# Eight PSUM banks for the first graph layer, and a hand-ordered tail with part of its rows on ScalarE and GpSimd

## The chip, the cores and the metric

The kernel runs on one core of a Trainium2 chip, in float32 almost throughout. The time is device microseconds (us) of that core, the median of several executions. Engines are named as the profile names them: PE (TensorE matmuls), PEld (TensorE weight loads), DVE (VectorE), ACT (ScalarE), POOL (GpSimd), SP (SyncE, which here only issues DMAs).

## What is computed

One transformer-like block over 1250 nodes with 768 features and 20000 edges. Cut to what matters:

```python
xn = layernorm(x)
x  = x + gnn(xn, edges) + linear_attention(xn)     # gnn: two graph attention layers, then @ Wu
y  = layernorm(x)
shared = silu(y @ ws_gate) * (y @ ws_up) @ ws_down
routed = sum over the 2 best of 8 experts of gate * expert(y)
out = x + alpha * shared + (1 - alpha) * routed     # alpha = sigmoid(y @ sg_w + sg_b)
```

A graph attention layer weighs, for each target node and head, the source nodes' rows by a softmax over the incoming edges: `out[dst] = sum(alpha * h[src])`. The first layer has 4 heads, the second 2.

## The kernel before, in words

Tokens are cut into ten tiles of 125 rows (`NT = 10`, `TP = 125`). `acc` (125 x 10 x 768, in SBUF) holds the running sum of the block and in the end the output. The stages follow each other: weights and counts of edges, linear attention, first graph layer, second graph layer with the product by Wu, routing, 22 blocks of expert work, and the tail. The order of instructions within each engine is set by a scheduler that keeps to dependencies; it may move instructions of one engine past each other, and each engine then runs its own list strictly in order. Waits are kept per tile: a write into a tile waits for the earlier reads of that tile, also when they touch another half of it. Two stages are touched.

**First graph layer** (`attend`, L582 to L603, with `step1` and `finish1`, L613 to L624). It runs over two halves of the targets (625 each) and four heads, so eight rounds, called heads below. A head takes ten steps, one for each tile of source nodes. In a step ACT makes two exponentials `ea` and `eb` (L593, L595; two buffers each), DVE takes their maximum (L596) and multiplies it by the edge counts into `u` (L598; three buffers), and PE adds u times G into five PSUM tiles `pa` (L615), one for each tile of 125 targets. A tile `pa` takes one of the eight PSUM banks. One `nc.tensor.matmul` of float32 shows as two MATMUL records, so a step is ten records, a head a hundred. When a head's ten steps are in, DVE takes for each of the five `pa` a reciprocal (L622) and a scaled sum into `h2` (L623), after which the bank is free. The pool `g1ps` (L612) has `NH2` = 5 banks: exactly one head's. Two further banks (`ps_m`, L444) are kept through both graph layers for small transposes `m_row` (L456), among them the ten that turn `h2` columns into the rows which the second layer starts from (`g_srow`, then a DMA out, a broadcast DMA back, and twenty maxima on DVE, L480).

**Tail** (L1108 to L1136). The expert blocks have scattered their rows into `ys` in DRAM. Ten DMAs on the SP queue (L1112) fetch for each token tile the two routed rows, `yg`, 768 KB each. For tiles 2 to 9, PE multiplies the shared expert's hidden rows by ws_down into `pds` (`shared`, L1047 to L1055): a tile `pds` has two halves of 384 columns in two banks, three tiles are in use, and a half is three matmuls (six records). DVE adds each half times `al` to `acc` (L1054). For each tile u, DVE adds its two routed rows times their gates (L1131), 768 columns each. A tile that is done is stored by two DMAs, 120 rows from the SP queue and 5 from the ACT queue (`store`, L1117 and L1118). Which of L1054 and L1131 comes first on DVE is left to the scheduler. The DMAs of SP and ACT take turns on eight completion semaphores, and a DMA waits until the one before it on its semaphore has landed.

Earlier in the kernel, GpSimd adds a bias to `acc` tile by tile (L402), 125 x 768 as well; VectorE works beside it.

Of the kernel before, what the change touches and what calls it, by code (L numbers as in the profile page):

```python
# [14 lines left out]
AF = mybir.ActivationFunctionType  # L15
ALU = mybir.AluOpType
AX = mybir.AxisListType
PSUM = bass.MemoryType.PSUM

P = 128  # L20
TP = 125
NT = 10
# [3 lines left out]
HALF = D // 2  # L26
# [35 lines left out]
def gps_block(ctx: ExitStack, tc: tile.TileContext, x, src, dst, norm_g, norm_b, W1, a_src1, a_dst1, b1,  # L62
              W2, a_src2, a_dst2, b2, Wu, bu, w_qkv, w_proj, b_proj, router_w, w_gate, w_up, w_down,
              ws_gate, ws_up, ws_down, sg_w, sg_b, out):
    nc = tc.nc
# [11 lines left out]
    acc = big.tile([TP, NT, D], F32, name="acc")  # L77
# [12 lines left out]
    ctx_g = ExitStack()  # L90
# [70 lines left out]
    with tc.tile_pool(name="ph1", bufs=1, reuse_waits="tile") as p1, tc.tile_pool(name="ph1w", bufs=2, reuse_waits="tile") as p1w, \  # L161
# [68 lines left out]
        for k in range(KD):  # L230
# [10 lines left out]
            for h in range(H1):  # L241
                o = (h % 2) * CG
                for i in range(2):
                    nc.tensor.matmul(pm[:, h // 2, o:o + CG], wt[:, 2 * h + i, :], w2x[:, 2 * h + i, :],
                                     start=(i == 0), stop=(i == 1))
            nc.scalar.activation(wg[:, k, :].rearrange("p (s c) -> p s c", s=2), pm[:, :, :2 * CG], AF.Copy,
                                 scale=gb[:, k:k + 1])
# [14 lines left out]
        for s in range(2):  # L262
            half = slice(s * HALF, (s + 1) * HALF)
            nc.tensor.matmul(pb2[:, s, :HALF], ones[:2, :], br[:, half], start=True, stop=False)
            for h in range(H2):
                nc.tensor.matmul(pb2[:, s, :HALF], bc[:, 24 + h:25 + h].to_broadcast([C2, TP]), wub[:, h, half], start=False,
                                 stop=(h == H2 - 1))
# [50 lines left out]
    with tc.tile_pool(name="cnt", bufs=1, reuse_waits="tile") as cp, \  # L318
# [74 lines left out]
        for t0 in range(0, NT, 2):  # L393
            ts = range(t0, t0 + 2)
            mv, r, r2 = ahead
            if t0 + 2 < NT:
                ahead = norm(t0 + 2)
            for i, t in enumerate(ts):
# [9 lines left out]
                for s in range(2):  # L408
                    ph = ps.tile([TP, 512], F32, name="ph", tag="mm", bufs=3)
                    for k in range(KD):  # L410
                        nc.tensor.matmul(ph[:, :2 * CG], xnT[:, k, tok], wg[:, k, s * 2 * CG:(s + 1) * 2 * CG],  # L411
                                         start=(k == 0), stop=(k == KD - 1))
# [12 lines left out]
        with tc.If(n_off > 0):  # L425
            for b0 in range(0, NB, 2):
# [3 lines left out]
                for c in range(ECH):  # L430
                    nc.vector.tensor_scalar(lof[c % 2], steps16[:, :TP], lo[:, c:c + 1], None, op0=ALU.is_equal)
                    nc.vector.tensor_scalar(wide[c % 2], steps16, relg[:, c:c + 1], None, op0=ALU.is_equal)
                    for i, pc in enumerate(pcs):
                        nc.tensor.matmul(pc[:, :BC], lof[c % 2], wide[c % 2][:, i * BC:(i + 1) * BC],
                                         start=(c == 0), stop=(c == ECH - 1))
# [5 lines left out]

    p3 = ctx_g.enter_context(tc.tile_pool(name="gat", bufs=1, reuse_waits="tile"))
    pmx = ctx_g.enter_context(tc.tile_pool(name="gatmax", bufs=2, reuse_waits="tile"))
    ps_m = ctx_g.enter_context(tc.tile_pool(name="gatps", bufs=2, space=PSUM, reuse_waits="tile"))  # L444

    W = N // 2
    NH2 = NT // 2
# [51 lines left out]
    with tc.tile_pool(name="ph2", bufs=1, reuse_waits="tile") as p2:  # L499
# [14 lines left out]
        with tc.tile_pool(name="kvw", bufs=2, side="right", reuse_waits="tile") as p2w, tc.tile_pool(name="kvps", bufs=2, space=PSUM, reuse_waits="tile") as ps:  # L514
# [4 lines left out]
            todo = [(h, t) for h in range(H1) for t in range(NT)]  # L519
# [62 lines left out]
    def attend(pw, ss, ss02, rrow, H, begin, step, finish, fill=lambda half: None):  # L582
        for half in range(2):
            for h in range(H):
                r = pmx.tile([P, 2, W], F32, name="r", tag="ssb")
                nc.sync.dma_start(r, bass.AP(tensor=rrow.tensor, offset=rrow.offset + h * N + half * W,
                                             ap=[[0, P], [H * N, 2], [1, W]]))
                sums = begin()
                for st in range(NT):


                    ea = pw.tile([TP, W], F32, name="ea", bufs=2)
                    nc.scalar.activation(ea, r[:TP, 0, :], AF.Exp, bias=ss[:, st, h:h + 1])  # L593
                    eb = pw.tile([TP, W], F32, name="eb", bufs=2)
                    nc.scalar.activation(eb, r[:TP, 1, :], AF.Exp, bias=ss02[:, st, h:h + 1])  # L595
                    nc.vector.tensor_max(ea, ea, eb)  # L596
                    u = pw.tile([TP, W], F32, name="u", bufs=3)
                    nc.vector.scalar_tensor_tensor(u, ea, 1.0, cntT[:, st, half * W:(half + 1) * W],  # L598
                                                   op0=ALU.min, op1=ALU.mult)
                    step(sums, st, h, u)  # L600
                    fill(half)
                finish(sums, half, h)
# [4 lines left out]
    with tc.tile_pool(name="h2p", bufs=1, reuse_waits="tile") as hp, tc.tile_pool(name="gatw", bufs=2, reuse_waits="tile") as pw:  # L607
# [1 line left out]

        with tc.tile_pool(name="g1ps", bufs=NH2, space=PSUM, reuse_waits="tile") as ps_a:  # L612
            def step1(pa, st, h, u):  # L613
                for i in range(NH2):
                    nc.tensor.matmul(pa[i][:, :CO + 1], u[:, i * TP:(i + 1) * TP], G[:, st, h, :CO + 1],  # L615
                                     start=(st == 0), stop=(st == NT - 1))

            def finish1(pa, half, h):
                for i in range(NH2):
                    t = half * NH2 + i  # L620
                    rd = pw.tile([TP, 1], F32, name="rd")
                    nc.vector.reciprocal(rd, pa[i][:, CO:CO + 1])  # L622
                    nc.vector.scalar_tensor_tensor(h2[:, t, :], pa[i][:, :CO], rd, b1w2 if h == 0 else h2[:, t, :],  # L623
                                                   op0=ALU.mult, op1=ALU.add)  # L624

            attend(pw, s1[:, :, 0, :], ss02, rrow, H1,
                   lambda: [ps_a.tile([TP, 512], F32, name="pa") for _ in range(NH2)], step1, finish1)
        h1pool.close()

        fp = ctx.enter_context(tc.tile_pool(name="ffn", bufs=1, side="right", reuse_waits="tile"))  # L630

        g2 = fp.tile([TP, NT, 2], F32, name="g2")
        al = fp.tile([TP, NT], F32, name="al")
# [158 lines left out]
    nh = HS // P  # L792
    xpool = ctx.enter_context(tc.tile_pool(name="xpool", bufs=1, side="right", reuse_waits="tile"))
    hTs_s = xpool.tile([P, nh, N], F32, name="hTs_s")
    wsd = xpool.tile([P, nh, D], F32, name="wsd")
# [10 lines left out]
    with tc.tile_pool(name="fln", bufs=2, reuse_waits="tile") as pw, tc.tile_pool(name="flnps", bufs=2, space=PSUM, reuse_waits="tile") as ps:  # L806
# [40 lines left out]
        for r in range(2):  # L847
# [5 lines left out]
            f = pw.tile([TP, NT], F32, name=f"r_f{r}", bufs=1)  # L853
# [25 lines left out]
        for e in range(NE):  # L879
# [3 lines left out]
                                       op0=ALU.mult, op1=ALU.add)  # L883
# [16 lines left out]
        for r in range(2):  # L900
# [7 lines left out]
            for t in range(NT):  # L908
                nc.tensor.matmul(pids[:, r * NBLK:(r + 1) * NBLK], spot[:, t, :], numb[:, t, :], start=(t == 0),
                                 stop=(t == NT - 1))  # L910
# [38 lines left out]
        for c0, cw in CHUNKS:  # L949
            for f in range(nh):  # L950
                pg = sps.tile([P, 512], F32, name="pg")
                pu = sps.tile([P, 512], F32, name="pu3")
                for pt, i in ((pg, 0), (pu, 1)):
                    for k in range(KD):
                        nc.tensor.matmul(pt[:, :cw], wsg[i][:, k, f * P:(f + 1) * P], xnT[:, k, c0:c0 + cw],
                                         start=(k == 0), stop=(k == KD - 1))
# [10 lines left out]
    with tc.tile_pool(name="fps", bufs=1, space=PSUM, reuse_waits="tile") as ps:  # L967
# [12 lines left out]
        pd = ps.tile([P, 2, 512], F32, name="pdb")  # L980
# [66 lines left out]
        def shared(t, banks):  # L1047

            for s, pt in enumerate(banks):
                half = slice(s * HALF, (s + 1) * HALF)  # L1050
                for f in range(nh):
                    nc.tensor.matmul(pt[:TP, :HALF], hTs_s[:, f, t * TP:(t + 1) * TP], wsd[:, f, half],  # L1052
                                     start=(f == 0), stop=(f == nh - 1))
                nc.vector.scalar_tensor_tensor(acc[:, t, half], pt[:TP, :HALF], al[:, t:t + 1], acc[:, t, half],  # L1054
                                               op0=ALU.mult, op1=ALU.add)  # L1055
# [9 lines left out]
        for j in range(NSURE):  # L1065
            more = j + 1 < NSURE
# [39 lines left out]
    blocks.close()  # L1106

    out_t = out.rearrange("(t p) d -> p t d", p=TP)  # L1108
    with tc.tile_pool(name="comb", bufs=1, reuse_waits="tile") as cb, tc.tile_pool(name="cps", bufs=3, space=PSUM, reuse_waits="tile") as ps:
        ygs = [cb.tile([P, 2, D], F32, name=f"yg{t}") for t in range(NT)]  # L1110
        for t in range(NT):
            nc.sync.dma_start(ygs[t], bass.AP(tensor=ys.tensor, offset=ys.offset + t * TP * D,  # L1112
                                              ap=[[D, P], [N * D, 2], [1, D]]))

        def store(t):

            nc.sync.dma_start(out_t[:TP - 5, t, :], acc[:TP - 5, t, :])  # L1117
            nc.scalar.dma_start(out_t[TP - 5:, t, :], acc[TP - 5:, t, :])  # L1118

        done = []  # L1120

        for t in range(2, NT):
            pd = ps.tile([TP, 2, 512], F32, name="pds")
            shared(t, [pd[:, s, :] for s in range(2)])
            if t == NT - 1:
                store(t)
            if t < 3:
                continue
            for u in range(2 * (t - 3), min(2 * (t - 3) + 2, NT)):
                for r in range(2):  # L1130
                    nc.vector.scalar_tensor_tensor(acc[:, u, :], ygs[u][:TP, r, :], g2[:, u, r:r + 1], acc[:, u, :],  # L1131
                                                   op0=ALU.mult, op1=ALU.add)
                if u < NT - 1:
                    done.append(u)
            while done and done[0] <= t:
                store(done.pop(0))  # L1136


# [25 lines left out]
```

## Time and profile before

| what | us |
|---|---|
| median of 3 runs (lowest, highest) | 1597.15 (1594.57, 1598.87) |
| the profiled execution | 1597.16 |
| its span, first to last instruction | 1595.1 |
| PE busy | 1525.0 (96% of the span) |
| DVE busy | 724.4 (45%) |
| ACT busy | 367.6 (23%) |
| POOL busy | 98.1 (6%) |
| mean granted TensorE clock | 0.985 |
| first graph layer, PE from first matmul to the last | 582.98 to 731.41 |
| stretch from there to the second layer's first step | 731.41 to 792.49 |
| tail, from its first matmul to the span's end | 1545.73 to 1595.1 |

How to read it: a row of the groups has line, engine, operation, output and inputs, and the count; then busy time and mean duration in ns; then the time for which the engine stood idle just before these instructions, and what ended it. A row of the timeline has the start, the time over which the merged instructions ran, engine, line, operation and count, and in brackets the idle time before it and what ended that. The last matmul's end in a group is modelled.

### The profile page before, as it was taken

The numbers are of one execution on the slowest core, as the hardware profiler recorded it, in microseconds if no ns is written. First come the engines' busy times: TensorE is split into PE (matmuls) and PEld (weight loads), VectorE is DVE, ScalarE is ACT, GpSimd is POOL, SyncE is SP. The second block draws the span as 40 slices with busy tenths as digits, with TensorE's granted clock in tenths as the row PEclk, the third lists the DMA queues.
The fourth block names the chain that finished last, engine by engine and source line by source line (L and its number), as shares of the span: only waits on it lengthen the run. The fifth ranks groups of instructions, "written<-read, shape, count | busy, mean of one in ns | idle before, by whom it ended". The sixth has DMA issues, their size and how long they took to land. (4 is left out here: it accounts for less than half of the span.)

```text
span 1595.1 us, 18670 instructions
## 1 busy us (share of the span) xinstructions
PE 1525.0 (96%) x7143; PEld 855.7 (54%) x7143; DVE 724.4 (45%) x1355; ACT 367.6 (23%) x630; POOL 98.1 (6%) x144
## 2 busy tenths in 40 slices
PE   5999889999999989999999999999999999999986
PEld 5666544444454669896555554444444444444443
DVE  7889639411535359996799651111111111111116
ACT  3222211111101048881276310101111010111100
POOL 2211000000000000000000100000100001000000
PEclk9999989999999999999999999999999999999998
DMA  7100031001201111002121343688888888888727
GB/s 202 40 1 1 2 132 65 7 0 50 63 10 50 40 46 33 33 17 78 33 62 49 108 176 151 218 316 321 301 311 317 317 308 307 307 326 312 265 101 270
DMA packets 92835, 229.18 MB, mean 144 GB/s; under 512 B 5431, under 2 KB 28061, under 8 KB 92742
## 3 DMA queue, kind: packets, MB, share of 16 engines
q1 hardware_dynamic: 84428, 199.30, 35.8%
q0 software_dynamic: 6112, 27.95, 5.0%
q8 instruction: 64, 1.05, 0.3%
q10 hardware_dynamic: 2202, 0.64, 0.2%
q14 instruction: 29, 0.24, 0.0%
HBM read 212.42 MB, written 16.43 MB: 143 GB/s over the span
## 5 line engine op out<-in xcount | busy, mean ns | idle before, releaser
L1012 PE MATMUL pgb<-wg,xT 128*64 128x384 f32 (+1 forms) x1056 | 178.8, 488 | 0.5 <-ACT xT L1019 0.5
L1012 PE MATMUL pdb<-wd,hT 128*64 128x384 f32 (+1 forms) x1056 | 175.1, 488 | 1.4 <-SPq L1092 1.4
L1012 PE MATMUL pub<-wu,xT 128*64 128x384 f32 (+1 forms) x1056 | 174.0, 486 | 0.0
L533 PE MATMUL pp<-wkv,xnT 128*125 128x512 f32 x360 | 160.8, 595 | 0.1
L615 PE MATMUL pa<-G,u 125*125 125x199 f32 x800 | 140.4, 336 | 11.2 <-DVE h L623 6.0
L615 PEld LDWEIGHTS pa<-G,u 125*125 125x125 f32 x800 | 135.6, 189 | 16.2 <-issue 7.2
L1012 PEld LDWEIGHTS pub<-wu,xT 128*64 128x64 f32 x1056 | 75.7, 137 | 94.5 <-issue 94.5
L1012 PEld LDWEIGHTS pdb<-wd,hT 128*64 128x64 f32 x1056 | 74.6, 137 | 91.6 <-issue 87.0
L1012 PEld LDWEIGHTS pgb<-wg,xT 128*64 128x64 f32 x1056 | 73.7, 137 | 90.7 <-issue 89.8
L533 PEld LDWEIGHTS pp<-wkv,xnT 128*125 128x125 f32 x360 | 65.6, 189 | 73.1 <-issue 72.7
L1031 DVE TENSOR_TENSOR h<-h,pgb 128x384 f32<-128x384 f32 x44 | 24.4, 554 | 171.7 <-ACT h L1030 171.7
L1042 DVE COPY y<-pdb 128x768 f32<-128x768 f32 x22 | 21.1, 958 | 178.8 <-PE pdb L1012 178.8
L411 PE MATMUL ph<-wg,xnT 128*125 128x400 f32 x240 | 99.6, 521 | 2.5 <-PEq L425 2.4
L598 DVE SCALAR_TENSOR_TENSOR u<-ea,cntT 125x625 f32<-125x625 f32 x120 | 93.9, 805 | 12.6 <-PE pa L615 8.0
L595 ACT ACTIVATE eb<-r,g_ss 125x625 f32<-125x625 f32 x120 | 95.0, 816 | 20.3 <-DVE ea L596 20.3
L596 DVE TENSOR_TENSOR ea<-ea,eb 125x625 f32<-125x625 f32 x120 | 94.0, 805 | 8.2 <-ACT ea L593 5.4
L480 DVE CUSTOM_DVE_ANT_0 junk<-ssb,absent 125x1250 bf16<-125x1250 f32 x60 | 87.8, 1463 | 11.7 <-DMA ssb<-g_srow_d 10.4
L1030 ACT ACTIVATE h<-pgb 128x384 f32<-128x384 f32 x44 | 21.6, 491 | 307.6 <-PE pgb L1012 307.6
L563 PE MATMUL pq<-xnT,wq 128*128 128x500 f32 (+1 forms) x216 | 82.6, 527 | 4.6 <-DMA wq<-in_L_mix_w_qkv_dram 4.5
L1036 DVE TENSOR_TENSOR h<-h,pub 128x384 f32<-128x384 f32 x44 | 24.4, 554 | 134.4 <-PE pub L1012 134.4
L715 PE MATMUL pu<-wu,xnT 128*125 128x384 f32 x240 | 82.1, 487 | 1.3 <-DVE acc L720 1.3
L576 PE MATMUL pu<-wp,at 128*125 128x384 f32 x240 | 80.4, 488 | 1.0 <-DVE acc L579 1.0
(267 smaller groups left out, 1666.9 us busy)
## 6 DMA issues: line engine op xcount, KB each, us to landing
wg<-in_L_ffn_w_gate_dram SPq DMA_DIRECT2D x22, 2304.0 KB, 8.4
wu<-in_L_ffn_w_up_dram SPq DMA_DIRECT2D x22, 2304.0 KB, 10.4
wd<-in_L_ffn_w_down_dram SPq DMA_DIRECT2D x22, 2304.0 KB, 9.6
yg<-ys SPq DMA_DIRECT2D x10, 768.0 KB, 9.4
r<-g_rrow_d SPq DMA_DIRECT2D x12, 625.0 KB, 4.0
wq<-in_L_mix_w_qkv_dram SPq DMA_DIRECT2D x18, 384.0 KB, 3.5
wkv<-in_L_mix_w_qkv_dram SPq DMA_DIRECT2D x6, 768.0 KB, 12.3
acc<-in_x_dram POOLq DMA_DIRECT2D x10, 375.0 KB, 10.6
```

The lines of the kernel that those rows point to most:

```text
L411: nc.tensor.matmul(ph[:, :2 * CG], xnT[:, k, tok], wg[:, k, s * 2 * CG:(s + 1) * 2 * CG], start=(k == 0), stop=(k == KD - 1))
L480: nc.vector.tensor_tensor_reduce(out=junk, in0=self.ssb[:TP], in1=absent[:, dt, :], scale=1.0, scalar=-3.0e38, op0=ALU.add, op1=ALU.max, a ...
L533: nc.tensor.matmul(pp, xnT[:, k, tok], wkv[:, k, :, :], start=(k == 0), stop=(k == KD - 1))
L563: nc.tensor.matmul(pq[:, :qw], wq[:, k, :], xnT[:, k, tok], start=(k == 0), stop=(k == KD - 1))
L576: nc.tensor.matmul(pu[:, s, :HALF], at[:, k, i * TP:(i + 1) * TP], wp[:, k, s * HALF:(s + 1) * HALF], start=(k == 0), stop=(k == KD - 1))
L595: nc.scalar.activation(eb, r[:TP, 1, :], AF.Exp, bias=ss02[:, st, h:h + 1])
L596: nc.vector.tensor_max(ea, ea, eb)
L598: nc.vector.scalar_tensor_tensor(u, ea, 1.0, cntT[:, st, half * W:(half + 1) * W], op0=ALU.min, op1=ALU.mult)
L615: nc.tensor.matmul(pa[i][:, :CO + 1], u[:, i * TP:(i + 1) * TP], G[:, st, h, :CO + 1], start=(st == 0), stop=(st == NT - 1))
L715: nc.tensor.matmul(pu[:, :HALF], xnT[:, k, t * TP:(t + 1) * TP], wus[s][:, k, :], start=(k == 0), stop=(k == KD - 1))
L1012: nc.tensor.matmul(pt[part, :HALF], rows[:, k, part], w[:, k, s * HALF:(s + 1) * HALF], start=(k == 0), stop=(k == KD - 1))
L1031: nc.vector.tensor_mul(h, h, pgs[s][:, :HALF])
```

## The change

Three things are done.

1. The first graph layer's pool gets eight banks instead of five. The two banks of `ps_m` are given back before the layer and taken anew, as pool `gatps2`, after it. So the ten `m_row` transposes of `h2` now stand behind the layer's last matmul; before, five of them stood among the matmuls of later heads. The scheduler also orders DVE and ACT somewhat differently within the heads, and PE takes a head's steps one after another, where it formerly took the first three steps bank by bank.
2. In the tail, every L1054 and every L1131 that stays on DVE is chained in the order in which it is written: five shared halves (tile 2, tile 3, the first half of tile 4), then in turn one routed row and one shared half.
3. For tiles 0 to 6 (`NSIDE` = 7) the second routed row leaves DVE: ACT scales it in place, and GpSimd adds it to `acc`; both wait for the DMA of that tile, the add also for DVE's first routed row of that tile, and the store of the tile waits for the add. DVE keeps 13 routed rows of 20.

The PE list in the tail has the same 48 matmuls; the second half of a tile still waits for DVE's read of the first half, and the order across tiles is much as before, with first halves a little further ahead: after tile 5's first half come tile 6's first half, 5's second, 7's first, one matmul of 8's first, 6's second, the rest of 8's first, two matmuls of 9's first, 7's second, the last of 9's first, and then the second halves of 8 and 9. On ACT five scalings stand ahead of the first store, and the last two among the stores. The fetches `yg` now take seven semaphores without a wait; the eighth, ninth and tenth wait for the first, third and fifth fetch. Before, the eighth and the tenth waited for the ACT queue's first and second store.

```diff
-    ps_m = ctx_g.enter_context(tc.tile_pool(name="gatps", bufs=2, space=PSUM, reuse_waits="tile"))
+    mps = ExitStack()
+    ps_m = mps.enter_context(tc.tile_pool(name="gatps", bufs=2, space=PSUM, reuse_waits="tile"))
...
-        with tc.tile_pool(name="g1ps", bufs=NH2, space=PSUM, reuse_waits="tile") as ps_a:
+        mps.close()
+        with tc.tile_pool(name="g1ps", bufs=8, space=PSUM, reuse_waits="tile") as ps_a:
...
         h1pool.close()
+        ps_m = ctx_g.enter_context(tc.tile_pool(name="gatps2", bufs=2, space=PSUM, reuse_waits="tile"))
...
+    line = []
+
+    def then(ins):
+        if line:
+            tc.add_manual_dep(ins.ins, line[-1].ins.name, mybir.DependencyInfo(
+                mybir.DependencyClass.NoSync, mybir.DependencyReason.SCHED_ONLY), reason="order")
+        line.append(ins)
...
+        def routed(u, r):
+
+            if r == 1 and u < NSIDE:
+                nc.scalar.activation(ygs[u][:TP, r, :], ygs[u][:TP, r, :], AF.Copy, scale=g2[:, u, r:r + 1])
+                nc.gpsimd.tensor_add(acc[:, u, :], acc[:, u, :], ygs[u][:TP, r, :])
+            else:
+                then(nc.vector.scalar_tensor_tensor(acc[:, u, :], ygs[u][:TP, r, :], g2[:, u, r:r + 1], acc[:, u, :],
+                                                    op0=ALU.mult, op1=ALU.add))
...
+        NSIDE = 7
+        todo = [(u, r) for u in range(NT) for r in range(2)]
+        side = [x for x in todo if x[1] == 1 and x[0] < NSIDE]
+        todo = [x for x in todo if x not in side]
...
+        def more(k):
+            nonlocal n
+            for u, r in todo[n:n + k]:
+                routed(u, r)
+                if r == 0 and u < NSIDE:
+                    routed(u, 1)
+                if r == 1 or u < NSIDE:
+                    store(u)
+            n += k
...
         for t in range(2, NT):
             pd = ps.tile([TP, 2, 512], F32, name="pds")
-            shared(t, [pd[:, s, :] for s in range(2)])
-            if t == NT - 1:
-                store(t)
-            if t < 3:
-                continue
-            for u in range(2 * (t - 3), min(2 * (t - 3) + 2, NT)):
-                for r in range(2):
-                    nc.vector.scalar_tensor_tensor(acc[:, u, :], ygs[u][:TP, r, :], g2[:, u, r:r + 1], acc[:, u, :],
-                                                   op0=ALU.mult, op1=ALU.add)
...
+            for s in range(2):
+                half = slice(s * HALF, (s + 1) * HALF)
+                for f in range(nh):
+                    nc.tensor.matmul(pd[:, s, :HALF], hTs_s[:, f, t * TP:(t + 1) * TP], wsd[:, f, half],
+                                     start=(f == 0), stop=(f == nh - 1))
+                then(nc.vector.scalar_tensor_tensor(acc[:, t, half], pd[:, s, :HALF], al[:, t:t + 1], acc[:, t, half],
+                                                    op0=ALU.mult, op1=ALU.add))
+                if t > 3:
+                    more(1)
+        more(len(todo) - n)
```

More of the change, by code (lines that the diff above doesn't have):

```diff
@@ L1118, in store @@
             nc.scalar.dma_start(out_t[TP - 5:, t, :], acc[TP - 5:, t, :])
-        done = []
+        def routed(u, r):
[9 more added lines that the diff above has]
+        todo = [x for x in todo if x not in side]
+        n = 0
+        def more(k):
[7 more added lines that the diff above has]
+            n += k
         for t in range(2, NT):
             pd = ps.tile([TP, 2, 512], F32, name="pds")
-            shared(t, [pd[:, s, :] for s in range(2)])
-            if t == NT - 1:
-                store(t)
-            if t < 3:
-                continue
-            for u in range(2 * (t - 3), min(2 * (t - 3) + 2, NT)):
-                for r in range(2):
-                    nc.vector.scalar_tensor_tensor(acc[:, u, :], ygs[u][:TP, r, :], g2[:, u, r:r + 1], acc[:, u, :],
-                                                   op0=ALU.mult, op1=ALU.add)
[L1133 to L1136, printed above, removed]
+            for s in range(2):
[8 more added lines that the diff above has]
+        more(len(todo) - n)
 _G, _M, _F = "L0_gnn_", "L0_mix_", "L0_ffn_"
```

## The prediction, written before the result was known

> **What bounds the kernel now.** The page first: PE is busy for 96% of the span, so only time in which PE stands still can be won, or time after its last matmul. In the groups by line I looked at what stood idle in the two stages.
>
> ```profile
> L615 PE MATMUL pa<-G,u 125*125 125x199 f32 x800 | 140.4, 336 | 11.2 <-DVE h L623 6.0
> ```
>
> The last field says that PE waited 11.2 us in this layer, most of it for L623, the read that frees a bank. The timeline of PE shows where:
>
> ```profile
> 620.89 5.29 PE L615 MATMUL pa<-G,u 125*125 125x199 f32 x30 [1.05 <-DVE h L623]
> 626.40 12.05 PE L615 MATMUL pa<-G,u 125*125 125x199 f32 x70 [0.23 <-DVE u L598]
> 639.51 5.29 PE L615 MATMUL pa<-G,u 125*125 125x199 f32 x30 [1.06 <-DVE h L623]
> ```
>
> A head starts every 18.62 us (639.51 - 620.89). Seventy records start over some 11.6 us, so the pitch is 0.1685 us and a head's hundred are 16.85: each boundary loses 1.78. The timeline of DVE shows what DVE needs for a head:
>
> ```profile
> 601.54 0.16 DVE L622 RECIPROCAL rd<-pa 125x1 f32<-125x1 f32 x1
> 601.62 0.80 DVE L596 TENSOR_TENSOR ea<-ea,eb 125x625 f32<-125x625 f32 x1
> 602.32 0.42 DVE L623 SCALAR_TENSOR_TENSOR h<-pa,rd,b1w 125x198 f32<-125x198 f32 x1
> 602.66 0.16 DVE L622 RECIPROCAL rd<-pa 125x1 f32<-125x1 f32 x1
> ...
> 628.68 1.52 DVE L598 SCALAR_TENSOR_TENSOR u<-ea,cntT 125x625 f32<-125x625 f32 x2
> ...
> 631.82 1.53 DVE L598 SCALAR_TENSOR_TENSOR u<-ea,cntT 125x625 f32<-125x625 f32 x2
> ```
>
> Two steps take 3.14 (631.82 - 628.68), so 1.57 each; a bank's reciprocal and sum with half a step's work between them take 1.12 (602.66 - 601.54).
>
> Last the tail, timeline of PE and DVE:
>
> ```profile
> 1545.73 7.33 PE L1052 MATMUL pds<-wsd,hTs_s 128*125 128x384 f32 x22 [0.92 <-PEq L1092]
> ...
> 1555.77 3.00 DVE L1131 SCALAR_TENSOR_TENSOR acc<-yg,g,acc 125x768 f32<-125x768 f32 x3 [7.21 <-DMA yg<-ys]
> ...
> 1559.88 22.10 PE L1052 MATMUL pds<-wsd,hTs_s 128*125 128x384 f32 x62 [6.82 <-DVE acc L1054]
> ...
> 1584.41 5.66 PE L1052 MATMUL pds<-wsd,hTs_s 128*125 128x384 f32 x12 [2.43 <-DVE acc L1054]
> ...
> 1590.11 0.62 DVE L1054 SCALAR_TENSOR_TENSOR acc<-pds,al,acc 125x384 f32<-125x384 f32 x1 [1.32 <-PE pds L1052]
> ```
>
> DVE stood at a routed row whose fetch had not landed, with a shared half queued behind it; PE waited 6.82 for that half, and 2.43 once more near the end. After both, the next six records took about 3.9 us where the steady pitch 0.3225 gives 1.94: PE ran at half clock, 2.0 lost each time. The span ends 4.4 after DVE's last end (1590.72).
>
> **Part 1, eight banks.** The stage runs 148.43 us (582.98 to 731.41). PE alone needs 8 x 16.85 = 134.8, and about 2.6 of half clock at the start, which stay: ceiling of the gain 11.0. The next limit is DVE with ACT: ten steps of 1.57, and five finishing cells of 1.12 which hold 2.5 steps, so 5.6 - 2.5 x 1.57 = 1.7 more: 17.4 a head. PE's first head took 18.8 (582.98 to 601.77), then 7 x 17.4 = 121.8: 140.6, a gain of 7.8. The three buffers of u hide a part of each finishing burst, so I take **9.0**, between 7.8 and 11.0. What is late next: DVE's sums and, for a head's fourth and fifth bank, L623 of the head before.
>
> The five transposes that move behind the layer are 0.16 us each, 0.8 on PE; they formerly filled boundary waits. Behind them stand the row's copy on ACT, the DMA out and back, and the twenty maxima, on whose last PE waits at 792.49. The new PE list also has one matmul (two records, 0.65) ahead of the last four transposes; the last L623 hides much of it. Between 0 and 1.4; I take **0.6 lost**. Nothing else in the second layer changes but where some L720 stand among the maxima; bounds -1 and +1, taken as 0, since PE has fill work there.
>
> **Part 2, the order on DVE.** Tiles 2 to 4's first half no longer queue behind a fetch: the 6.82 and its 2.0 of half clock go. The first routed row starts as before, at about 1556.2 (its fetch lands at 1555.7). Fetches then land every 2.0 (DVE's and SP's waits before: 1555.7, 1557.7, 1559.6) and DVE needs one only every 1.9 or slower. The new semaphores send the eighth and tenth earlier: nothing, since those rows come last. But the wait within a tile stays: a second half needs DVE's read of the first, and that now stands in a fixed place between routed rows.
>
> **Part 3, rows moved.** DVE loses 7 x 0.93 = 6.5 us (pitch of L1131). ACT's scaling of 768 columns is estimated at 0.95 from L595's 0.82 for 625; ACT is idle, a fetch's landing precedes it, and only its own later scalings and small stores queue behind it: nothing. The add on GpSimd has an exact row, L402, the same shape, 1.81. This is what it does to DVE, on the timeline:
>
> ```profile
> 74.94 1.81 POOL L402 TENSOR_TENSOR acc<-acc,bias 125x768 f32<-125x768 f32 x1 [0.89 <-DVE xn L401]
> 75.12 0.17 DVE L127 RECIPROCAL ln_rs<-ln_rs 125x2 f32<-125x2 f32 x1
> 75.33 1.43 DVE L128 TENSOR_TENSOR ln_rs<-ln_rs 125x2 f32<-125x2 f32 x1
> ```
>
> A product of 125 x 2 elements takes 1.43 and ends with the add. The Trainium skill (SBUF — State Buffer, "SBUF: two separate sides") says why: GpSimd and a DVE operation with two SBUF inputs take turns on one port pair, held for a whole instruction. By it a routed row, which reads yg and acc, waits; a shared half, whose one input is PSUM, doesn't (L415, of that form, kept its 0.63 beside an add). So routed row and add alternate: 1.01 + 0.06 to hand over (an estimate) + 1.65 of holding (75.33 + 1.43 less the product's own 0.11, from 74.94, rounded down, as other blocked rows got through 0.15 early) = 2.7 a tile, where PE would give 1.94. Without the rule the cell is 0.93 + 0.53 = 1.46 and PE's pace decides.
>
> By hand along the new lists, with 2.7: the first routed rows start at 1556.2, 1559.4, 1562.2, 1564.9, 1567.6, 1570.3, 1573.0; the last add ends at about 1575.8. From tile 6 on PE waits for the read of a first half: 0.7, then 0.9 for tile 7, then from 1574.5 to 1577.3 for tile 8, and some 2.2 to 4 for tile 9. DVE's last four shared halves and five routed rows follow: last routed row at 1586.3 with no half clock, 1588.2 with one stretch of it, 1590.2 with two. The skill (TensorE: Matmul & The Clock Gate, "What's actually happening") wants a whole idle window of about 3.4 us for the drop, so none after waits of 2.6 and 2.2; but 2.43 cost 2.0 here, and 1.06 in the layer above did not. The waits lie near 2.43; I take one drop: 1588.2 + 4.4 = 1592.6 for the span's end, **2.5 gained** in the tail, of bounds 0.5 and 4.5. Parts 2 and 3 thus give back most of 6.82 + 2.43 + 4.0: PE's wait for a late DMA becomes a wait for a DVE that waits for GpSimd.
>
> **Sum**, against the profiled execution's 1597.16 (span 1595.1; the median 1597.15 is the same): 9.0 - 0.6 + 2.5 = 10.9. Predicted 1586.3.
>
> **Rivals.**
> - *The port costs little* (the add lets routed rows through, or the order of arrival is kinder): then cells follow PE. By the same hand list the last routed row ends at 1583.5 to 1585.5, the tail gains 5.3 to 7.3, with the layer 9.0 to 9.5: total 13.7 to 16, 1581 to 1583.5. For it: shared halves pass, so only seven rows can be held. Against it: every two-input row beside L402 was held. 0.22.
> - *DVE and ACT become the layer's bound and PE goes cold twice in the tail.* 7.8 - 0.6 + 0.5 = 7.7: 1589.5, to 1592.5 if the maxima shift too. For it: DVE is at 17.4 a head against 16.85. Against it: DVE idles 0.17 a pair now. 0.16.
> - *Slower, by the adds on GpSimd alone.* Seven adds each hold up a row, and everything after is DVE's list. To lose the layer's 8.4 and 4.8 more, the adds must cost 13.2 + 2.5 = 15.7 beyond my sum, 2.2 each: a holding time of about 3.9 in place of 1.65. It decides from there; L402's longest, begun behind a DVE row, was 2.16. Time then 1602 or above. 0.03.
> - *The banks do nothing*, if the next head's first matmuls still wait at L623: then only the tail's 2.5 less 0.6, 1595.3. The PE list's waits are per tile and the first three of a head's banks were freed two heads ago, so 0.03.
>
> **How the numbers follow.** My forecast has 0.56, its own range 1583.5 to 1589.5. The range 1580.5 to 1591.5 takes in the first rival and most of the second. A measurement of this kernel tells 0.3%, 4.8 us, from no change. Faster by more than that, below 1592.4: 0.56 + 0.22 + 0.10 of the second rival, 0.88; within: 0.09; slower: 0.03.
>
> **What would show it.** In the layer heads start every 17 to 17.4 us, and the wait for L623 at a head's first matmul is gone. In the tail the 6.82 is gone; L1131's successor shows durations of 1.6 to 2.7 in place of 1.01 while GpSimd adds, cells of 2.7, and two PE waits of 2 to 3 us late on, for the shared halves. Wrong if the routed rows keep 1.01 beside the adds, if GpSimd's adds take over 2.2, if heads stay at 18 or more, or if fetches and stores on the DMA queues end last.

## The result and the profile after

The changed kernel takes 1587.88 us (median of 5 runs, 1586.79 to 1589.16) in place of 1597.15: a ratio of 0.9946, 95% interval 0.9933 to 0.9958, so 9.3 us faster. 1586.3 was forecast. The profiled execution took 1586.79, span 1584.9. The traces of both, cut at the same events (the first matmul of each stage on PE):

| stretch | before | after | forecast of the difference |
|---|---|---|---|
| start to the first graph layer | 582.98 | 581.65 | 0 |
| first graph layer | 148.44 | 140.93 | -9.0 |
| from there to the second layer's first step | 61.08 | 62.54 | +0.6 |
| second layer, routing, experts | 753.24 | 753.31 | 0 |
| tail | 49.41 | 46.43 | -2.5 |

The first row has nothing to do with the change: over the profiled runs below that start lies between 580.36 and 583.83, in no order that follows the edits. So experiments are judged by stretch, and small differences of whole times are not read at all.

**The layer.** The page's row of its matmuls (before: 140.4 busy, 11.2 idle, of which 6.0 for L623):

```profile
L617 PE MATMUL pa<-G,u 125*125 125x199 f32 x800 | 138.5, 336 | 6.0 <-DVE u L599 3.4
```

The 3.4 put down to `u` is the wait ahead of the layer's very first matmul (3.38), and before's 11.2 holds the same wait (3.47). Between the first matmul and the last, PE's idle time fell from 7.7 to 2.6, and at a head's first matmul there is no wait for a bank any more. The timeline of PE after shows the waits that are left, here behind the fourth head's start (634.05):

```profile
635.53 0.57 PE L617 MATMUL pa<-G,u 125*125 125x199 f32 x2 [0.30 <-DVE rd L624]
636.64 18.64 PE L617 MATMUL pa<-G,u 125*125 125x199 f32 x109 [0.54 <-DVE rd L624]
```

These are the head's fourth and fifth banks, which the head before still holds until its sums (L625) have read them, at 635.38 and 636.50; the profile names the reciprocal beside them. The next boundary has no such wait: heads start at 600.27, 617.22, 634.05, 652.26, 669.09, 687.31 and 704.28, alternately 16.8 to 17.0 and 18.2 apart, 17.5 on average.

**The tail**, timelines of PE, DVE and POOL after:

```profile
1553.28 1.82 POOL L1136 TENSOR_TENSOR acc<-acc,yg 125x768 f32<-125x768 f32 x1 [1.41 <-DVE acc L1138]
1553.59 2.32 DVE L1138 SCALAR_TENSOR_TENSOR acc<-yg,g,acc 125x768 f32<-125x768 f32 x1
1556.34 1.81 POOL L1136 TENSOR_TENSOR acc<-acc,yg 125x768 f32<-125x768 f32 x1 [1.25 <-DVE acc L1138]
1556.65 2.31 DVE L1138 SCALAR_TENSOR_TENSOR acc<-yg,g,acc 125x768 f32<-125x768 f32 x1
...
1570.57 2.20 PE L1164 MATMUL pds<-wsd,hTs_s 128*125 128x384 f32 x6 [2.66 <-DVE acc L1166]
1575.06 3.07 PE L1164 MATMUL pds<-wsd,hTs_s 128*125 128x384 f32 x6 [2.29 <-DVE acc L1166]
```

The 6.82 of before is gone. Where an add runs on GpSimd a routed row (L1138) takes 2.03 to 2.32 in place of 1.01 (six rows), and ends 0.8 after the add (1553.59 + 2.32 against 1553.28 + 1.82). Without further waits a cell of row, add and shared half is 2.76. PE waits twice late, for DVE's read of a first half. In the last two rows six records take 2.20 after a wait of 2.66, at full clock, and 3.07 after one of 2.29: the granted clock is 0.50 from 1576.25 on.

### The profile page after: what moved, and what is told of

It reads as the page before. It is cut to its first block, busy times and chain, and to the rows that moved or that the text cites. A ratio compares the mean times of both kernels' runs of the same rounds, so it can differ in the third digit from the quotient of the medians.

```text
span 1584.9 us, 18678 instructions
## 1 busy us (share of the span) xinstructions
PE 1518.2 (96%) x7143; PEld 851.3 (54%) x7143; DVE 728.6 (46%) x1348; ACT 374.8 (24%) x637; POOL 109.3 (7%) x151
## 5 line engine op out<-in xcount | busy, mean ns | idle before, releaser
L718 PE MATMUL pu<-wu,xnT 128*125 128x384 f32 x240 | 83.5, 493 | 0.9 <-DVE acc L723 0.9
```

The costliest lines, as they stand in the source:

```text
L718: nc.tensor.matmul(pu[:, :HALF], xnT[:, k, t * TP:(t + 1) * TP], wus[s][:, k, :], start=(k == 0), stop=(k == KD - 1))
```

## Experiments

Times are medians, ratios are to the kernel before on the same chip.

### Each part alone

e1_banks has the diff's lines on `mps`, `g1ps` and `gatps2` and the old tail; e2_tail has the new tail and five banks.

> The eight banks alone, the tail as before. If the two parts add up: the layer gives 7.5 us (148.4 to 140.9, as in the changed kernel), the stretch to the second layer's first step takes back 1.5 (62.7 in place of 61.3), the tail stays at 49.4: 1591.2, ratio 0.9962. If the changed tail made some of the gain in the layer, or the layer's gain is lost before the tail, 1593 or more.

> The tail alone, five banks in the layer. If the parts add up: tail 46.5 us in place of 49.4, layer 148.4, together 1594.3, ratio 0.998; the routed rows that follow an add on GpSimd show about 2.3 us in place of 1.01.

Measured: e1_banks 1591.34, ratio 0.995 (0.9932 to 0.9968), layer 140.94, next stretch 63.73, tail 50.56. e2_tail 1594.61, ratio 0.998 (0.9973 to 0.9988), layer 148.44, next stretch 60.79, tail 46.54. The layer and the new tail come out as in the changed kernel, so the parts add up there, and the loss between the layers belongs to the banks, since e2_tail has none. Two stretches of e1_banks are longer than that sum. Its tail, though the same code as before, took 1.15 more: behind the same long wait of PE the half clock covered 5.9 us of matmuls (to 1560.72) in place of 3.7. Its next stretch is 1.2 longer than the changed kernel's, for which there is no experiment.

### The rows moved to GpSimd

```diff
-        NSIDE = 7
+        NSIDE = 0
```

> The changed kernel with no row moved to ScalarE and GpSimd: DVE keeps all 20 routed rows, in the order by hand. Port theory (GpSimd's adds hold up DVE's routed rows): every routed row is back at 1.01, a cell of routed row and shared half at 1.46, and DVE's tail ends 20 x 0.93 + 11 x 0.53 = 24.5 us after the first row starts, 5 to 8 us earlier than with seven rows moved: 1580 to 1583. Rival (the moved rows are a real relief, DVE's own work decides): seven rows more on DVE cost 6.5 us: about 1594.

e4_noadd leaves out the seven adds on GpSimd, so the second routed row of tiles 0 to 6 is missing from its sums; the scalings on ACT stay.

> The changed kernel with GpSimd's seven adds left out (the second routed row of tiles 0 to 6 is scaled but not added). Port theory: the 13 routed rows stay at 1.01, no row is held, the tail follows PE and its waits within a tile: last row about 4 us earlier than in the changed kernel, 1582 to 1584, not much better than with no row moved. Rival (rows are long because of the fetches or ScalarE's scaling, both still there): rows stay at 2.3 and the time stays within 1 us of 1587.9.

Measured: e3_side0 1590.47, ratio 0.996 (0.9946 to 0.9974), tail 50.05: as neither theory had it. e4_noadd 1584.34, ratio 0.9924 (0.9902 to 0.9946), tail 43.72, 2.7 less than after. Rows take 1.01 in both, so the adds do hold the rows up. e4_noadd lies just above the 1582 to 1584 of the port theory, but 6.1 under e3_side0, where little difference had been expected. This is e3's timeline of DVE:

```profile
1553.88 0.62 DVE L1166 SCALAR_TENSOR_TENSOR acc<-pds,al,acc 125x384 f32<-125x384 f32 x1 [1.52 <-PE pds L1164]
1554.42 1.01 DVE L1138 SCALAR_TENSOR_TENSOR acc<-yg,g,acc 125x768 f32<-125x768 f32 x1
...
1572.87 8.94 DVE L1138 SCALAR_TENSOR_TENSOR acc<-yg,g,acc 125x768 f32<-125x768 f32 x9
```

DVE, no longer blocked, stands 1.52 in every second cell waiting for PE, and nine rows are left when the halves are done. The order allows one row to a half, and PE cannot hurry, since a second half waits for DVE's read of the first. My sum for e3 had assumed that DVE never waits. So a second suspect came up beside the port: the wait within a tile.

### A bank to each shared half

```diff
-            pd = ps.tile([TP, 2, 512], F32, name="pds")
             for s in range(2):
+                pd = ps.tile([TP, 512], F32, name="pds")
```

The pool has six buffers then, so the same six banks.

> The changed kernel, with each shared half in a PSUM tile of its own bank (six buffers) in place of two halves in one tile. Theory: PE's late waits of 0.89, 0.74, 2.66 and 2.29 in the tail are waits of a tile's second half for VectorE's read of the first half; with a bank to each half PE runs ahead and they go, while the seven cells of 2.7 with GpSimd's adds stay, so VectorE's list alone sets the end: first routed row at about the same place, seven cells of 2.76, then the remaining rows and halves without gaps, tail 42 to 43.5 in place of 46.4, time 1583.5 to 1585. Rival (PE's waits only mirror a VectorE that is the bound already, so removing them moves nothing): tail 46 to 46.5, time 1587 to 1588.

Measured: 1582.24, ratio 0.991 (0.9894 to 0.9927), tail 42.22. PE's timeline is one row, and DVE's has no wait after its second row:

```profile
1537.97 31.20 PE L1164 MATMUL pds<-wsd,hTs_s 128*125 128x384 f32 x96 [0.90 <-PEq L1095]
```
```profile
1558.49 2.31 DVE L1138 SCALAR_TENSOR_TENSOR acc<-yg,g,acc 125x768 f32<-125x768 f32 x1
1560.72 0.60 DVE L1166 SCALAR_TENSOR_TENSOR acc<-pds,al,acc 125x384 f32<-125x384 f32 x1
1561.25 2.31 DVE L1138 SCALAR_TENSOR_TENSOR acc<-yg,g,acc 125x768 f32<-125x768 f32 x1
```

The rival, that PE's waits only mirror a full DVE, falls: the tail lost 4.2 us with the shared tile. Of this 0.9 is the half clock behind one of its waits; against e11_six below, which has the changed kernel's tail without that drop (45.57), it is 3.35. The cells of 2.76 stay.

### All rows on DVE, two to a half

```diff
-        NSIDE = 7
+        NSIDE = 0
...
-                    more(1)
+                    more(2)
```

on top of e5_split.

> As e5_split, with no row moved to ScalarE and GpSimd (NSIDE 0) and two routed rows of VectorE after each shared half from tile 4 on, in place of one. Theory (the port makes a moved row cost 1.3 in wait for the 0.93 it saves net of the row it replaces, so VectorE with all twenty rows back needs no more than with seven adds): cells of 2 x 0.93 + 0.53 = 2.39, rows 1.0 throughout, no GpSimd in the tail; tail 40 to 42, time 1580.5 to 1583. Rival (the rows moved are a true relief, VectorE's list is too long without it): tail 46 or longer, time 1587.5 or more.

Measured: 1586.12, ratio 0.9933 (0.9915 to 0.9952), tail 45.27. That looks like the rival, but DVE waited 4.07 and 3.15, both before a shared half and both named `DMA out_dram<-acc`. Two rows to a half reach tile 8 before its second half and tile 9 before both: their stores went ahead of those sums (which are therefore missing from the output), and the sums had to wait until the stores had read. A fault of this edit's order, not a fact about the rows. Mended with `more(min(2, 2 * (t + s) - n))`:

> As e8_split_two, with the order mended: a tile's routed rows come only after both of its shared halves, so that no store of a tile precedes its sums and the last two tiles are complete in the output. Theory (VectorE's list is the bound of the tail once each half has its bank, and a row moved to GpSimd saves it nothing): eight cells of 2 x 1.0 + 0.53 = 2.5 from 1548.5 on, then four halves of 0.53 and four rows of 1.0, no wait of VectorE after the first row; tail 39.5 to 41.5, time 1578.5 to 1581.5, a little under e5_split. Rival (the moved rows do relieve VectorE): slower than e5_split's 1582.2.

Measured: 1581.73, ratio 0.9905 (0.9886 to 0.9924), tail 40.97:

```profile
1554.24 2.06 DVE L1138 SCALAR_TENSOR_TENSOR acc<-yg,g,acc 125x768 f32<-125x768 f32 x2
1556.22 0.61 DVE L1166 SCALAR_TENSOR_TENSOR acc<-pds,al,acc 125x384 f32<-125x384 f32 x1
1556.75 2.06 DVE L1138 SCALAR_TENSOR_TENSOR acc<-yg,g,acc 125x768 f32<-125x768 f32 x2
```

A cell of two rows and a half takes 2.51, less than the 2.76 of one row, a half and a turn of GpSimd. In e12_two_ok the layer, too, was shorter, 140.29, because it began at full clock. The whole times of e5 and e12 are not told apart; the tails of their traces, 42.22 and 40.97, are. In e12 no second row runs on ACT or GpSimd: with DVE's list free of gaps, moving rows away gains nothing.

### What holds the layer at 17.5 a head

e7_max500 takes work from DVE; e9_layer_order changes its order (and gives the reciprocals four buffers): `finish1` is written as reciprocal, reciprocal, sum, sum, the first two `u` of the next head are made ahead of it, and all of it is chained.

```diff
+                w_ = 425 if H == H1 else W
...
-                    nc.vector.tensor_max(ea, ea, eb)
+                    nc.vector.tensor_max(ea[:, :w_], ea[:, :w_], eb[:, :w_])
```

> The changed kernel, with the first graph layer's maximum of the two exponentials taken over only 425 of 625 columns (it leaves out the maximum for 200 columns of every step, nothing else): 0.2 us less for VectorE in each of 80 steps, 2 us a head. Theory (VectorE's sum of 17.4 a head is the bound of the layer with eight banks, PE needs 16.85): heads fall to 16.9, layer 137 to 138 in place of 140.9, time 3 to 4 us less, 1584 to 1585. Rival (the order in which the banks come free decides, whatever VectorE's load): heads stay at 17.5 mean, layer 140.5 to 141, time 1587 to 1588.5.

> The changed kernel, with VectorE's order in the first graph layer written out by hand: the next head's first two factors are made ahead of a head's finish, and the five reciprocals and sums of a finish then follow each other in pairs with nothing between them; same instructions in number and kind. Theory (VectorE's sum is the bound): layer 139.5 to 142, no gain to speak of, time 1586.5 to 1589. Rival (only the order matters: PE waits at every second head for its fourth and fifth bank because the scheduler put steps between the sums): the waits at heads 3, 5 and 7 go, layer about 137.5, time about 1584.5.

Measured: e7_max500 1584.98, ratio 0.9921 (0.9904 to 0.9937), layer 136.75, next stretch 63.23, heads of 16.83 from the third on: PE's own pace. e9_layer_order 1596.45, ratio 0.9995 (0.9986 to 1.0004), layer 147.11, heads of 18.5 to 18.8 from the third on. Both expectations missed for e9, which lost 6.2 in the layer. Its timeline of DVE tells why:

```profile
613.87 0.81 DVE L657 TENSOR_TENSOR ea<-ea,eb 125x625 f32<-125x625 f32 x1
614.78 0.81 DVE L659 SCALAR_TENSOR_TENSOR u<-ea,cntT 125x625 f32<-125x625 f32 x1
615.50 0.80 DVE L657 TENSOR_TENSOR ea<-ea,eb 125x625 f32<-125x625 f32 x1
...
617.14 0.23 DVE L634 RECIPROCAL rd<-pa 125x1 f32<-125x1 f32 x2
...
619.40 0.80 DVE L657 TENSOR_TENSOR ea<-ea,eb 125x625 f32<-125x625 f32 x1
```

A product directly behind the maximum that feeds it mostly starts 0.91 after it (0.84 in a head's first step), where the others of this size start 0.72 to 0.73 after their neighbour: a strictly alternating step takes 1.63. Ten of them and a finish of 2.26 (619.40 - 617.14) are 18.6, about the head that was measured. In the changed kernel such an alternating stretch precedes every second boundary, and the head behind it is the one of 18.2; that the one makes the other is not shown.

### Six banks

```diff
-        mps.close()
-        with tc.tile_pool(name="g1ps", bufs=8, space=PSUM, reuse_waits="tile") as ps_a:
+        with tc.tile_pool(name="g1ps", bufs=6, space=PSUM, reuse_waits="tile") as ps_a:
```

with the pool `ps_m` kept open as before.

> The changed kernel with six banks for the first layer's sums in place of eight, and the two banks of the maxima's pool left open beside them as in the kernel before. Theory (the 1.5 lost between the layers comes from giving the maxima's banks to the sums, so that the five transposes cannot be done inside the layer; and one spare bank covers only one matmul of 0.17 of a boundary): stretch between the layers back to 61.0 to 61.5, layer 146 to 148, tail 46.4, time 1592 to 1595. Rival (the stretch between the layers is longer for another reason, such as a later start of the row behind VectorE's last sums): it stays at 62 to 63; and if one spare bank already lets VectorE's list decide, the layer is 141 to 143.

Measured: 1588.73, ratio 0.9949 (0.9931 to 0.9967), layer 141.34, next stretch 61.08, tail 45.57. One spare bank does nearly all that three do in the layer: the theory was wrong there by 5 to 7 us, and the rival's last clause was right. From the third head on heads take 17.4 to 17.5, the last 18.4, with no alternation. Five transposes `m_row` run inside the layer again; the first:

```profile
653.70 5.04 PE L615 MATMUL pa<-G,u 125*125 125x199 f32 x28 [0.25 <-DVE u L598]
658.57 0.27 PE L456 MATMUL m_row<-ident,h 125*2 125x125 f32 x1
658.68 3.53 PE L615 MATMUL pa<-G,u 125*125 125x199 f32 x20
```

And the stretch behind the layer is back at the 61.08 of before. Its edit against the changed kernel is the pools alone, so the loss there came with the transposes' banks. The last experiment shows by which way: what counts is where the transposes stand, not the banks as such.

### Both, and deeper buffers

e13_both joins e11_six and e12_two_ok.

> The two edits that gained beyond the changed kernel, together: six banks for the first layer's sums with the maxima's pool left open (e11_six), and in the tail a bank to each shared half, all routed rows on VectorE, two to a half (e12_two_ok). If they add: layer 141.3, between the layers 61.1, tail 41.0, so the span is 1584.9 + (141.3 - 140.9) + (61.1 - 62.6) + (41.0 - 46.4) = 1578.4, time about 1580.3, 1578.5 to 1582 with the spread of the start. Rival (the stretch between the layers was short in e11_six by chance): between the layers 62 to 63, time 1581.5 to 1583.

Measured: 1580.01, ratio 0.9888 (0.9871 to 0.9904); layer 141.34, next stretch 60.87, tail 40.98: it adds, and beats both kernels. The timelines of ACT and DVE in the six-bank layer (here e11's, the same code in this layer) led to the last experiment:

```profile
628.43 1.54 ACT L595 ACTIVATE eb<-r,g_ss 125x625 f32<-125x625 f32 x2 [0.16 <-DVE ea L596]
629.87 1.54 ACT L593 ACTIVATE ea<-r,s 125x625 f32<-125x625 f32 x2
```
```profile
630.72 1.53 DVE L596 TENSOR_TENSOR ea<-ea,eb 125x625 f32<-125x625 f32 x2 [0.17 <-ACT ea L593]
632.17 1.52 DVE L598 SCALAR_TENSOR_TENSOR u<-ea,cntT 125x625 f32<-125x625 f32 x2
```

ACT waits 0.16 for DVE and DVE 0.17 for ACT in every pair of steps. Neither is full; they hand two buffers back and forth. The second layer's steps share the edited lines:

```diff
-                    ea = pw.tile([TP, W], F32, name="ea", bufs=2)
+                    ea = pw.tile([TP, W], F32, name="ea", bufs=4)
...
-                    eb = pw.tile([TP, W], F32, name="eb", bufs=2)
+                    eb = pw.tile([TP, W], F32, name="eb", bufs=4)
```

> As e13_both, with four buffers in place of two for each of the exponentials ea and eb. In six banks the trace shows ScalarE and VectorE waiting for each other by turns, 0.16 and 0.17 a pair of steps, and ScalarE standing 0.2 to 0.6 at a time while VectorE finishes a head; VectorE's own instructions sum to 20 x 0.7275 + 5 x 0.41 = 16.6 a head, under TensorE's 16.85, where the step of 1.57 that the sum of 17.4 was made of is this exchange and not VectorE's work. Theory (the two buffers, not VectorE's work, make the 17.4): heads fall to 16.9 to 17.1, layer 137 to 138.5, time 1576.5 to 1578. Rival (VectorE's sum as it was put, or the scheduler's order on it, decides): heads stay at 17.3 to 17.6, layer 140.5 to 142, time 1579.5 to 1581.

Measured: 1576.74, ratio 0.9882 (0.9864 to 0.99), layer 138.03, heads of 18.59, 17.35, 17.14 and from then on 16.99. PE:

```profile
617.78 37.47 PE L615 MATMUL pa<-G,u 125*125 125x199 f32 x218
```

For 37 us, over two whole heads, PE has no wait that the timeline lists, and it has none in the rest of the layer either. The gain of 3.3 is clear in the layer; 1.4 of it is the last head (18.35 before this edit). In the whole time it is not: the intervals of e13 and e14 overlap. From the second layer's first step to the tail it took 751.83 against e13's 753.32. The stretch between the layers was longer, 62.12 against 60.87, and PE's timeline shows the changed kernel's picture there:

```profile
719.36 0.80 PE L456 MATMUL m_row<-ident,h 125*2 125x125 f32 x6
720.00 0.81 PE L715 MATMUL pu<-wu,xnT 128*125 128x384 f32 x2
720.65 0.59 PE L456 MATMUL m_row<-ident,h 125*2 125x125 f32 x4
...
766.01 1.12 PE L456 MATMUL m_row<-ident,g_rc 125*4 125x125 f32 x6 [2.00 <-DVE g_rc L493]
766.92 1.49 PE L715 MATMUL pu<-wu,xnT 128*125 128x384 f32 x2
```

The scheduler put all ten transposes behind the layer, though their two banks were there all the time. It also ordered DVE's list differently than in e13. So the edit did more than add buffers.

## Why the prediction held, step by step

**The layer: 9.0 forecast, 7.5 measured, just below the lower bound of 7.8.** Seven heads at 17.5 follow a first of 18.6; the sum "17.4 a head" was nearly the measured pace. The term that was mis-sized is the credit of 1.2 for "the three buffers of u hide a part of each finishing burst": it did not show, and the heads took 0.1 more on average than the sum without it. The reason under the sum was also wrong. "The next limit is DVE with ACT: ten steps of 1.57" read a pace as a need: 1.57 is the exchange over two buffers. DVE's own work is 20 instructions at a pitch of 0.72 to 0.73 (e14's, where it isn't waiting) plus, for each of five banks, 0.08 for a reciprocal and 0.33 for a sum: 16.6 a head, below PE's 16.85. e7 was compatible with either reading. e14 leaves all of DVE's work in place, and the pace falls from 17.4 to 17.0: so the amount of that work was not the limit. Whether the buffers alone did it, or the other order on DVE that came with them, is not separated; the listed waits of DVE went from four of some 0.17 a head to one, about the 0.4 that the head gained.

Two readings under this sum were off. "PE waited 11.2 us in this layer" takes in the 3.47 ahead of it. And "about 2.6 of half clock at the start" is 1.7: e12, which began at full clock, had a first head of 16.93 in place of 18.61.

**What is late next.** "For a head's fourth and fifth bank, L623 of the head before" is what PE waits for at 635.53 and 636.64 (the sums are L625 now). But six banks show that this matters little: there the second to the fifth bank must all be freed by the head before, and the layer is 0.4 longer.

**Between the layers: 0.6 lost forecast, 1.46 measured.** All ten transposes and a matmul among them (the 0.85 at 724.04) now stand behind the layer's last matmul:

```profile
722.58 0.48 PE L457 MATMUL m_row<-ident,h 125*2 125x125 f32 x3
723.73 0.48 PE L457 MATMUL m_row<-ident,h 125*2 125x125 f32 x3 [0.66 <-DVE h L625]
724.04 0.85 PE L718 MATMUL pu<-wu,xnT 128*125 128x384 f32 x2
724.73 0.59 PE L457 MATMUL m_row<-ident,h 125*2 125x125 f32 x4
...
770.05 0.82 PE L457 MATMUL m_row<-ident,g_rc 125*4 125x125 f32 x6 [2.00 <-DVE g_rc L494]
770.69 1.46 PE L718 MATMUL pu<-wu,xnT 128*125 128x384 f32 x2
```

The last transpose ends 2.7 behind the layer's last matmul (725.32), before 1.7. Of that difference of 1.1, 0.5 arrived at the transposes of the maxima (770.05 - 722.58 = 47.47, before 46.94). From there to the second layer's first step it took 15.07, before 14.14: the other 0.9 goes with two L718 records of 1.46 in place of 0.81, the half clock behind a wait of 2.00 (before 1.48). The other traces agree:

| transposes behind the layer | runs | wait | slow records | stretch |
|---|---|---|---|---|
| five | before, e2, e11, e13 | 1.47 or 1.48 | no | 60.79 to 61.08 |
| ten | e3, e4, e9, e12 | 2.00 | no | 61.55 to 61.92 |
| ten | after, e1, e5, e7, e8, e14 | 2.00 | yes | 62.12 to 63.73 |

So 0.5 to 1.1 goes with the transposes, near the 0.6 forecast, and the rest with a drop of the clock, for which the sum had no term. It comes in six of the ten runs that have the wait of 2.00, and which ones is a matter of chance (last section).

**The tail: 2.5 forecast, 2.98 measured.** The 6.82 went, cells were 2.76 where 2.7 was said, and PE's late waits 2.66 and 2.29 where 2.6 and 2.2 had been read from the list. The last routed row ended 42.47 after the tail's first matmul (1578.82 + 2.07 - 1538.42), exactly where the forecast's 1588.2 has it (1588.2 - 1545.73). That is luck. One drop of half clock came as taken, but it cost 0.9 (3.07 - 2.20) and not 2.0, so without it the list was about 1.0 slower than the 1586.3 of the forecast. And that it was one is chance: with the same tail code it is none in e11 (tail 45.57), one in after, e2 and e7 (46.43 to 46.65), two in e9 (48.38). The 0.5 gained beyond the forecast lies behind the last row: 4.0 to the end of the span in place of 4.4. "2.0 lost each time" was also misread: the line of twelve records in 5.66 is 1.6 over the steady 11 x 0.3225 + 0.49.

The step "a second half needs DVE's read of the first" was right and weighed too little: e5 shows 4.2 us in it, 3.35 without the drop, and the adds are 2.7 (e4). The sentence that parts 2 and 3 give back most of what they win is what the runs show.

**The rivals.** That the port costs little is refuted by the rows of 2.03 to 2.32 and by e4. That the banks do nothing is refuted by e1. The case of a DVE-bound layer was right in size (140.93, where 140.6 was worked out) but not in its two clock drops. Nothing slower was seen.

**The sum.** 10.9 was forecast and 9.3 measured. Two of the three terms lie outside their own bounds, both on the bad side (7.5 under 7.8, 1.46 over 1.4), and the wide range held the sum. Of the 10.2 between the two profiled executions' spans, 1.3 is the earlier start of the layer, chance as far as these runs go; the stages give 7.5 - 1.46 + 2.98 - 0.07 = 8.95.

## What to carry to other kernels

When two engines hand tiles to each other, a steady pace is not yet either one's need: look for small waits on both sides (0.16 and 0.17 here), add up the instructions without them, and try a deeper buffer before moving work. When two profiles differ by a microsecond behind a wait of PE, look at the granted clock first: here the same code and the same wait came with a drop and without one. Before giving a stage more banks, try one spare bank, and look at who worked in the banks that are taken away; and split a tile in two where its second half waits for the reader of the first. A row moved to GpSimd is only a saving if VectorE doesn't then wait for it: here one row with an add cost 2.76 a cell, two rows on VectorE alone 2.51.

## What the runs showed of the hardware

- A VectorE row with two SBUF inputs that starts beside a GpSimd add takes 2.03 to 2.32 in place of 1.01 (after) and ends some 0.8 after the add's recorded end, as if its own work came last; a shared half, one of whose inputs is in PSUM, ran in 0.60 to 0.62 throughout. That is the shared port of the forecast; unexpected was only how exactly the cell of 2.76 repeats.
- On VectorE an instruction directly behind the one whose result it reads starts 0.91 after it, 0.18 to 0.19 later than behind an independent one (125 x 625, e9). An order by hand that alternates them lost 6.2 us in the layer.
- PE's half clock doesn't follow the length of a wait but where the wait falls. In all 14 traces the granted clock changes only at whole windows of 3.41 us, counted from a point that differs from run to run: after drops at 582.97, is back at 586.38, drops at 770.70 and is back at 774.11, so 3.41 each time, with 184.32 = 54 x 3.413 between. A drop goes with the time for which PE has no matmul within one such window:

| wait of PE | window of 3.41 us | idle in it | clock in the next window |
|---|---|---|---|
| before, 2.43 until 1584.41 | 1580.69 to 1584.11 | 2.13 | 0.5 |
| after, 2.29 until 1575.06 | 1572.83 to 1576.25 | 2.23 | 0.5 |
| e11, 2.29 until 1574.88 | 1573.07 to 1576.49 | 1.80 | 1.0 |
| after, 2.66 until 1570.57 | 1566.01 to 1569.42, and the next | 1.51, 1.21 | 1.0 |
| after, 2.00 until 770.05 | 767.29 to 770.70 | 2.00 | 0.5 |
| e12, 2.00 until 771.60 | 769.75 to 773.16 | 1.85 | 1.0 |

From 500 us on, the 14 traces have 37 windows at full clock that a drop followed, each with 2.00 or more of idle PE, and 4350 that none followed, each with 1.96 or less. Earlier, with other matmuls, eight drops came at less idle time, so the limit is read for this part of the kernel alone, and no experiment was made to move it. The Trainium skill (TensorE: Matmul & The Clock Gate, "What's actually happening") asks for at least one idle window of about 3.4 us before the drop, in windows that run freely and don't restart with the kernel. The free-running windows are what these traces show. That a window must be idle as a whole is not: no wait in the table fills one, and three of them dropped the clock. There the measurement decides.
